# A message-passing layer on one core: node stage in two passes, section ends in the loop, one-hot offsets in PSUM

## The chip, the core and the metric

The kernel runs on one core of a Trainium2 chip. Six things work side by side on that core: TensorE (PE in the profile: matrix products and transposes, with its weight loads listed as PEld), VectorE (DVE), ScalarE (ACT), GpSimd (POOL), SyncE (SP, which here only issues transfers) and 16 DMA engines that move data between device memory and the on-chip SBUF. TensorE writes to PSUM, a small memory from which VectorE and ScalarE read the results. The engines run their own queues in order and wait for each other through semaphores.

The metric is the device time of one execution in microseconds, lower is better. Several runs are made; the median is what is compared.

## The reference

12500 nodes with 128 features, 400000 edges sorted by their target node. A pre-normalised graph layer: normalise and rectify the node features, make a message for each edge from its two ends, weight it by a small network of the edge's attributes, turn it into eight heads' scores and values, take a softmax over all edges with the same target, sum, project, and add the input.

```python
h = relu(layernorm(x))                             # 12500 x 128
msg_src = h @ w_src + b_src
msg_dst = h @ w_dst
message = msg_src[src] + msg_dst[dst]              # 400000 x 128
rad_w   = silu(silu(edge_attr_32 @ fc_w1 + fc_b1) @ fc_w2 + fc_b2) @ fc_w3 + fc_b3
message = message * edge_weight1 * rad_w
m_h     = (message @ w_sep + b_sep).reshape(E, 8, 32)
alpha, value = smooth_leaky_relu(m_h[:, :, :16]), m_h[:, :, 16:]
score   = einsum("ehk,hk->eh", alpha, alpha_dot)
att     = segment_softmax(score, dst)              # per target node and head
out     = segment_sum(value * att[..., None], dst).reshape(12500, 128) @ w_proj + b_proj
return x + out
```

## The kernel before, in words

**Node stage (L147-347).** The 12500 nodes lie in 98 tiles of 128 rows, taken four at a time (25 quads). For each quad: statistics on VectorE (`stats`, L213), normalise and rectify on ScalarE (`norm`, L227 and the lines behind it), transposes on TensorE with a copy to SBUF on VectorE (`turn`, L240-243), then products of each tile with both weight matrices side by side, 128 x 256 (`products`, L246, matmul L255), copies out of PSUM, mostly ScalarE (L261), and stores of the source product to `t_src` and of the target product to `t_dst` (L266). Between quads stand pieces of other work: `load_targets` (L176), `load_weights` (L189, one after the other on SP's queue), `fits` (L271: compares neighbouring targets, L273, and counts the falls, L276, to decide whether the fast path may be taken) and `cuts` (L302: marks where the target changes).

**The loop (`windows`, L662).** The edges are cut into 800 sections of 500, two sections make a step, 400 steps. A section's targets fall in a window of 64 nodes. Step k, an order written out by hand (`step`, L972 and on), works on several edges' stages at once: loads for later steps, the gather of source rows for step k+2, the edge network for k+2 to k, the messages of k, the scores of k-1, and, 13 steps later (LAG), the values and sums of step c = k - 13.

- `prep_load`, `prep_make`, `prep_turn` (L675-706): for every 16 steps, the source indices `idx` and the offsets `loc` of each edge's target from the first target of its section, turned by TensorE into the tile misc in PSUM and copied by VectorE to SBUF.
- `gather` (L742): POOL issues indirect transfers of 128 rows each out of `t_src` (L749), 3125 in all, into buffers `gs0` and `gs1`, three of each.
- `mlp1` (L763, matmuls L768 into the PSUM tiles `m1` and `misc`, run in two row halves of TensorE), `mlp2`, `mlp3`, `radial` (L802, VectorE L807), `sources` (L810, L819 and L822: gathered rows turned into PSUM), `message` (L825, VectorE L835), `alphas` (L838, matmul L840, VectorE L847), `scores` (L850).
- Softmax over eight steps at a time (k mod 8): running maxima up and down, each one VectorE scan of 500 columns (L875, L880), the exponentials (`softmax_exp`, L883), and their transposes into misc (`softmax_T`, L895).
- `one_hot` (L909): VectorE compares the offsets `loc` with a row of lane numbers (L913, 125 x 504) and, for the last column of each window, with the offset of the section's last target (L916, 125 x 8). `values` (L920, product L926, VectorE L928), `sums` (L933: TensorE with the one-hot as weights into misc, L937; ScalarE copy L941), then stores to a window table and to `agg`.
- In steps 40 to 239 also `load_x` and `add_x` (L952-964): input plus output bias, stored as `xb`; in the first steps the zeroing of `agg`, two transfers a step.

[...]

**After the loop (L1069-1220).** A node's edges may be split over sections, so the first and last row of every section, 1600 section ends, are combined: 13 blocks of 128 ends. Within drain steps 400 to 415 the jobs do this for all ends at once: load the ends and their maxima (L1085, L1098), scan for the common maximum (L1126), factors (L1132-1137), transposes of the ends' rows (L1143-1150), scans that sum them (L1157), quotients (L1162-1164), transposes back, and 13 scatters by POOL into `agg` (L1175).

**Final stage (L1251-1340), behind the branch.** Loads of `xb` on ScalarE's queue and of `agg` on SP's (L1268), quotients (L1279-1282), transposes (L1293), the projection (L1304), on VectorE the value bias for nodes that have edges (L1308, one instruction a tile) and the sum (L1312), and the stores of the output.

L352-660 hold a second path for other inputs, which is not taken here.

Of the kernel before, what the change touches and what calls it, by code (L numbers as in the profile page):

```python
# [30 lines left out]
P = 128  # L31
C = 128
# [24 lines left out]
def gnn_kernel(ctx: ExitStack, tc: tile.TileContext, a: dict, out: bass.AP):  # L57
# [20 lines left out]
    win = dram.tile([NS * W, ROW], F32, name="win")  # L78
    ends_d = dram.tile([1, 2 * NS + 2], I32, name="ends_d")
# [46 lines left out]
    dst_h = dst.rearrange("(k f e) -> f k e", f=2, e=SEC)  # L126
# [22 lines left out]
    with tc.tile_pool(name="node", bufs=2) as np_, tc.tile_pool(name="node1", bufs=1) as n1, \  # L149
# [15 lines left out]
        CC = E // P  # L165
        cur = n1.tile([P, CC + 1], I32, name="cur")
# [9 lines left out]
        def load_targets():  # L176

            nc.sync.dma_start(out=cur[:, 1:CC + 1], in_=dst.rearrange("(p c) -> p c", p=P))
            at = dst[CC - 1:CC]
            with nc.allow_non_contiguous_dma(reason="single targets"):  # L180
                nc.sync.dma_start(out=cur[1:P, 0:1], in_=bass.AP(at.tensor, at.offset, [[CC, P - 1], [1, 1]]))
                for f in range(2):
                    nc.sync.dma_start(out=base[:, f, :], in_=dst_h[f:f + 1, :, 0])
# [4 lines left out]
        def load_weights():  # L188
            for name, t in wt.items():  # L189
# [5 lines left out]
                nc.sync.dma_start(out=t, in_=ap)  # L195
            for f in range(2):
                for q in range(2):
                    o = (2 * q + f) * RAD
                    nc.sync.dma_start(out=w1b[o:o + RAD, f * FC:(f + 1) * FC], in_=a["fc_w1"])
                s = slice(f * FC, (f + 1) * FC)  # L200
                for q in range(2):
                    nc.sync.dma_start(out=w2b[s, q * FC:(q + 1) * FC], in_=a["fc_w2"])
                nc.sync.dma_start(out=w3b[s, :], in_=a["fc_w3"])
                nc.sync.dma_start(out=b12[s, 0:1], in_=a["fc_b1"])
                nc.sync.dma_start(out=b12[s, 1:2], in_=a["fc_b2"])
# [6 lines left out]
        hs, hTs = {}, {}  # L212
        G = 8  # L213
        def stats(t0, t1):
            for t in range(t0, t1):
# [3 lines left out]
                nc.vector.bn_aggr(mv[:n, t, :], st[:n])  # L219
            s = slice(t0, t1)  # L220
# [13 lines left out]
        def turn(i):  # L234
# [6 lines left out]
            hTs[i] = np_.tile([P, 4, P], F32, name="hT", bufs=3)  # L241
            w = (t1 - t0 - 1) * P + rows(t1 - 1)
            nc.vector.tensor_copy(hTs[i].rearrange("p u n -> p (u n)")[:, :w],
                                  pt.rearrange("p u n -> p (u n)")[:, :w])

        def products(i):  # L246
            t0, t1 = quads[i]
            hT = hTs.pop(i)
            ms = np_.tile([P, 2, 4, C], F32, name="ms", bufs=6)
            for v0 in range(t0, t1, 2):  # L250
                vs = range(v0, min(v0 + 2, t1))
                pm = nps.tile([P, 2, 2, C], F32, name="pm", bufs=4)
                for t in vs:
                    n = rows(t)
                    nc.tensor.matmul(pm[:n, t - v0], hT[:, t - t0, :n], w_nodes, start=True, stop=True)  # L255
                for n, u0, u1 in blocks(v0, vs[-1] + 1):
                    o, q = ms[:n, :, u0 - t0:u1 - t0, :].rearrange("p k j c -> p j k c"), pm[:n, u0 - v0:u1 - v0]
                    if v0 % 16 == 2:
                        nc.vector.tensor_copy(o, q)
                    else:  # L260
                        nc.scalar.copy(o, q)  # L261
            f1 = min(t1, NF)
            for k, table in enumerate((t_src, t_dst)):
                tv = table[0:NF * P, :].rearrange("(p t) c -> p t c", t=NF)
                if t0 < f1:
                    nc.sync.dma_start(out=tv[:, t0:f1, :], in_=ms[:, k, 0:f1 - t0, :])  # L266
                if t1 > NF:
                    nc.sync.dma_start(out=table[NF * P:N, :], in_=ms[:tail, k, NF - t0, :])


        def fits():  # L271
            gt = n1.tile([P, CC], BF16, name="gt")
            nc.vector.tensor_tensor(gt, cur[:, 0:CC], cur[:, 1:CC + 1], op=ALU.is_gt)  # L273
            cnt = n1.tile([P, 2], F32, name="cnt")
            nc.vector.memset(cnt, 0.0)
            nc.vector.tensor_reduce(cnt[:, 0:1], gt, AX.X, ALU.add)  # L276
# [3 lines left out]
            nc.vector.tensor_reduce(cnt[:100, 1:2], span, AX.X, ALU.add)  # L280
            tot = nps.tile([1, 1], F32, name="tot", bufs=1)
            for j in range(2):
                nc.tensor.matmul(tot, cnt[:, j:j + 1], ones[:, 0:1], start=(j == 0), stop=(j == 1))
            nc.vector.tensor_copy(bad, tot)
# [9 lines left out]


# [7 lines left out]
        def cuts():  # L303
# [16 lines left out]
            nc.vector.tensor_scalar(b_s, pb, 0.25, None, op0=ALU.mult)  # L320
            nc.vector.tensor_sub(far, eb[:, :, 1], eb[:, :, 0])
# [5 lines left out]
        stats(0, 4)  # L327
        norm(0)
        stats(4, G)
        norm(1)  # L330
        turn(0)
        for i in range(Q):
            if i % 2 == 0 and 4 * i + G < NB:
                stats(4 * i + G, min(4 * i + 2 * G, NB))
            if i + 2 < Q:
                norm(i + 2)
            if i + 1 < Q:
                turn(i + 1)
            products(i)
            if i == 5:  # L340
                load_targets()
            if i == 9:
                load_weights()
            if i == 15:
                fits()
            if i == 20:
# [314 lines left out]
    def windows():  # L661
# [5 lines left out]
        with tc.tile_pool(name="wk2", bufs=2) as sp, tc.tile_pool(name="ps", bufs=1, space=PSUM) as pp, \  # L667
                tc.manual_schedule(), ExitStack() as held:
            lp = held.enter_context(tc.tile_pool(name="ld", bufs=2))
            prep, e_g, d_g, w_g, md, gath = {}, {}, {}, {}, {}, {}  # L670
            eTs, h1s, h2s, ohT, m3, mr, mTs, als, S_all, sms, Ps, Pem, pvx, ohs, accs, xs, Ms, pms, p3s, rads = (
                {} for _ in range(20))


            def prep_load(u):  # L675
# [10 lines left out]
                prep[u] = (ri, rb)  # L686

            def prep_make(u):
                ri, rb = prep[u]
                rows = lp.tile([P, 2, P], F32, name="rows", bufs=1)  # L690
                rf = lp.tile([P, 1], F32, name="rf", bufs=1)
                nc.vector.tensor_copy(rf, rb)
                nc.vector.tensor_copy(rows[:T, 0, :], ri[:T, 0, :])
                nc.vector.tensor_scalar(rows[:, 1, 0:T], ri[:, 1, 0:T], rf, None, op0=ALU.subtract)
                prep[u] = rows

            def prep_turn(u):
                rows = prep[u]
                pt = pp.tile([P, 2, P], F32, name="misc")
                nc.tensor.transpose(pt[:, 0, 0:T], rows[:T, 0, :], ident[:T, :T])  # L700
                nc.tensor.transpose(pt[:T, 1, :], rows[:, 1, 0:T], ident)
                idx = lp.tile([P, T], I32, name="idx")
                nc.vector.tensor_copy(idx, pt[:, 0, 0:T])
# [38 lines left out]
            def gather(k, f):  # L742
                gs = lp.tile([P, TS, C], F32, name=f"gs{f}", bufs=3)
                u = k // 16
                idx, _ = prep[u]
# [17 lines left out]
            def mlp1(k):  # L763

                p1 = [pp.tile([P, 2 * T], F32, name=n) for n in ("m1", "misc")]
# [107 lines left out]
            def softmax_up(m):  # L873
                Ms[m] = sp.tile([P, 2, SEC], F32, name="M")
                nc.vector.tensor_tensor_scan(Ms[m][:, 0, :], sms[m][:, 0:SEC], S_all[m], RESTART,  # L875
                                             op0=ALU.add, op1=ALU.max)

            def softmax_down(m):
                M = Ms[m]
                nc.vector.tensor_tensor_scan(M[:, 1, ::-1], sms[m][:, SEC:0:-1], M[:, 0, ::-1], RESTART,  # L880
                                             op0=ALU.add, op1=ALU.max)
# [13 lines left out]
            def softmax_T(m):  # L895
                pt = pp.tile([T, TS, P], F32, name="misc")
                for t in range(TS):
                    nc.tensor.transpose(pt[:, t, :], Ps[m][:, t * T:(t + 1) * T], ident)
                Pem[m] = sp.tile([T, TS, MQ, H], F32, name="Pem")
                nc.scalar.copy(Pem[m].rearrange("p t q h -> p t (q h)"), pt)  # L900
# [8 lines left out]
            def one_hot(c):  # L909
                _, loc = prep[c // 16]  # L910
# [22 lines left out]
            def sums(c):  # L933
                acc = pp.tile([P, ROW], F32, name="misc")
# [12 lines left out]
            def store(c, f):  # L947
                at = nc.sync.value_load(base[0:1, f, c:c + 1])
                nc.sync.dma_start(out=agg[ds(at, W - 1), :], in_=accs[c][f * W:(f + 1) * W - 1, :])


            def load_x(i):  # L952
                xs[i] = lp.tile([P, 4, C], F32, name="xs")
# [5 lines left out]
            def add_x(i):  # L959
                t = xs.pop(i)  # L960
                for n, t0, t1 in blocks(*quads[i]):
                    u = t[:n, t0 - quads[i][0]:t1 - quads[i][0], :]
                    nc.vector.tensor_tensor(u, u, b_out[:n].unsqueeze(1).to_broadcast([n, t1 - t0, C]), op=ALU.add)
                    nc.sync.dma_start(out=xb_v[:, t0:t1, :] if n == P else xb[NF * P:N, :].unsqueeze(1), in_=u)

# [3 lines left out]
            prep_load(0)  # L969
            prep_make(0)  # L970
            prep_turn(0)
            for k in range(2):  # L972
                load_e(k)
            def step(k):
                c = k - LAG
                if has(c - 2):
# [3 lines left out]
                if k % 16 == 4 and has(k + 12):  # L980
                    prep_load((k + 12) // 16)
                if has(k + 3):
# [7 lines left out]
                if has(c - 2):  # L990
# [4 lines left out]
                if k % 16 == 8 and has(k + 8):  # L995
                    prep_turn((k + 8) // 16)
                if k % 16 == 7 and has(k + 9):
# [4 lines left out]
                if 0 <= i < Q and q == 7:  # L1002
                    add_x(i)
                if has(k + 1):
# [27 lines left out]
                if has(c):  # L1032
                    values(c, 1)
# [330 lines left out]
```

## Time and profile before

| what | value |
|---|---|
| median of 3 runs | 4316.28 us (4314.72 to 4322.2) |
| the profiled execution, its own time | 4315.26 us |
| its span (first to last instruction) | 4313.4 us |
| granted TensorE clock, mean | 0.977 |
| node stage, TensorE's first to last product | 9.0 to 108.2 us |
| first source matmul of step 15, of step 399 | 302.7, 4109.2 us |
| loads of `agg` for the final stage | 4229.7 us |
| data moved | 790.10 MB, 183 GB/s |

The page lists each engine's busy time, then the busy share in 40 equal slices of some 108 us:

```profile
PE   6679999999999999999999999999999999999974
...
DVE  7357777777777777777777777777777777777776
ACT  6335555555455455455555455454555545544521
POOL 0667777777777777777777777777777777777701
PEclk8789999999999999999999999999999999999987
DMA  5667777777777777777777777777777767777725
```

One digit is a slice, 9 meaning 90% busy or more: the first slice is the node stage, the next one or two the start of the loop, the last one the end of the section ends and the final stage; all between is the loop. In the other views a line gives the engine, the line of the kernel, the operation, and the tiles as out<-in. A group's line ends with its busy time, the mean duration in ns, and after the second bar the engine's idle time just before these instructions, with what ended it.

### The profile page before, as it was taken

The numbers are of one execution on the slowest core, as the hardware profiler recorded it, in microseconds if no ns is written. First come the engines' busy times: TensorE is split into PE (matmuls) and PEld (weight loads), VectorE is DVE, ScalarE is ACT, GpSimd is POOL, SyncE is SP. The second block draws the span as 40 slices with busy tenths as digits, with TensorE's granted clock in tenths as the row PEclk, the third lists the DMA queues.
The fourth block names the chain that finished last, engine by engine and source line by source line (L and its number), as shares of the span: only waits on it lengthen the run. The fifth ranks groups of instructions, "written<-read, shape, count | busy, mean of one in ns | idle before, by whom it ended". The sixth has DMA issues, their size and how long they took to land.

```text
span 4313.4 us, 91919 instructions
## 1 busy us (share of the span) xinstructions
PE 4065.7 (94%) x31567; PEld 2626.4 (61%) x31567; DVE 3101.8 (72%) x5980; ACT 2105.5 (49%) x4995; POOL 3037.4 (70%) x3148
## 2 busy tenths in 40 slices
PE   6679999999999999999999999999999999999974
PEld 5346666666666666666666666666666666666653
DVE  7357777777777777777777777777777777777776
ACT  6335555555455455455555455454555545544521
POOL 0667777777777777777777777777777777777701
PEclk8789999999999999999999999999999999999987
DMA  5667777777777777777777777777777767777725
GB/s 207 196 183 183 183 193 184 192 194 185 194 188 186 192 190 186 192 183 185 198 186 193 185 177 190 183 182 185 175 181 188 177 182 184 182 185 178 173 59 190
DMA packets 598603, 790.10 MB, mean 183 GB/s; under 512 B 125595, under 2 KB 475424, under 8 KB 597996
## 3 DMA queue, kind: packets, MB, share of 16 engines
q1 hardware_dynamic: 394314, 520.94, 43.1%
q0 software_dynamic: 100416, 205.45, 23.2%
q10 hardware_dynamic: 103394, 57.74, 5.1%
q8 instruction: 250, 4.10, 0.4%
q14 instruction: 229, 1.88, 0.1%
HBM read 643.48 MB, written 140.67 MB: 182 GB/s over the span
## 4 chain that ended last, share of the span: by engine, by line
PE 80%; DMA 8%; ACT 3%; DVE 3%; issue 2%; POOL 2%; SPq 1%; ACTq 0%; POOLq 0%; DVEq 0%
PE V L926 16%; PE pa L840 14%; PE misc L937 9%; PE pm L829 6%; PE p L800 6%; PE pm L819 6%; PE p L783 5%; PE m L768 5%; PE m L854 4%; PE pm L822 4%; DMA gs<-t_src,idx 4%; POOL gs L749 2%; PE m L759 2%; ACT L842 1%; DMA agg<-z 1%
## 5 line engine op out<-in xcount | busy, mean ns | idle before, releaser
L749 POOL DMA_INDIRECT gs<-t_src,idx x3125 | 3023.0, 967 | 1082.9 <-issue 778.6
L842 ACT ACTIVATE sl<-pa,c_b_a 128x500 f32<-128x500 f32 x800 | 541.8, 677 | 1004.4 <-PE pa L840 996.8
L926 PEld LDWEIGHTS V<-c_w_v,mT 128*125 128x125 f32 x6192 | 735.3, 188 | 479.8 <-DVE ohT L793 231.9
L928 DVE TENSOR_TENSOR pvx<-V,Pem 125x512 f32<-125x512 f32 x774 | 530.9, 686 | 524.2 <-PE V L926 495.5
L926 PE MATMUL V<-c_w_v,mT 128*125 128x128 f32 x6192 | 875.3, 285 | 0.2 <-DVE pvx L928 0.2
L840 PE MATMUL pa<-mT,c_w_a 128*128 128x500 f32 x1600 | 817.4, 593 | 53.8 <-DVE al L847 51.8
L847 DVE SCALAR_TENSOR_TENSOR al<-pa,sl 128x500 f32<-128x500 f32 x800 | 542.3, 678 | 239.6 <-ACT sl L842 227.0
L822 PEld LDWEIGHTS pm<-ident,gs 128*128 128x128 f32 x2350 | 418.6, 192 | 380.0 <-issue 359.5
L807 DVE SCALAR_TENSOR_TENSOR rad<-p,c_fc_b,w_b 128x500 f32<-128x500 f32 x800 | 553.3, 733 | 104.2 <-PE p L800 101.4
L835 DVE SCALAR_TENSOR_TENSOR mT<-pm,c_b_src,rad 128x500 f32<-128x500 f32 x800 | 553.2, 733 | 79.9 <-PE pm L829 66.1
L937 PE MATMUL misc<-pvx,oh 125*64 125x136 f32 x6400 | 463.7, 288 | 0.0
L937 PEld LDWEIGHTS misc<-pvx,oh 125*64 125x64 f32 x6400 | 361.1, 138 | 163.7 <-ACT eT L761 157.3
L819 PE MATMUL pm<-ident,gs 128*128 128x128 f32 (+9 forms) x2725 | 436.9, 275 | 13.1 <-DMA gs<-t_src,idx 12.7
L800 PE MATMUL p<-h,w3b 64*128 64x500 f32 x1600 | 406.5, 585 | 11.1 <-ACT h L786 11.1
L786 ACT ACTIVATE h<-p,b 128x500 f32<-128x500 f32 x400 | 326.3, 816 | 177.1 <-PE p L783 134.5
L941 ACT COPY ob<-misc 128x136 f32<-128x136 f32 x400 | 108.9, 272 | 618.3 <-PE misc L937 533.7
L822 PE MATMUL pm<-ident,gs 128*128 128x12 f32 (+30 forms) x2350 | 384.2, 244 | 16.5 <-DMA gs<-t_src,idx 15.7
L819 PEld LDWEIGHTS pm<-ident,gs 128*128 128x128 f32 (+9 forms) x2725 | 339.2, 157 | 30.2 <-DMA gs<-t_src,idx 18.3
L829 PE MATMUL pm<-ohT,m 64*128 64x500 bf16 x2400 | 325.6, 378 | 0.0
L840 PEld LDWEIGHTS pa<-mT,c_w_a 128*128 128x128 f32 x1600 | 243.1, 192 | 81.4 <-DVE al L847 65.6
L768 PE MATMUL m<-eT,w1b 64*128 64x250 f32 x800 | 276.7, 426 | 7.5 <-ACT Sp L857 6.5
L768 PE MATMUL misc<-eT,w1b 64*128 64x250 f32 x800 | 276.7, 426 | 0.0
(151 smaller groups left out, 4227.0 us busy)
## 6 DMA issues: line engine op xcount, KB each, us to landing
w_b<-in_edge_weight SPq DMA_DIRECT2D x400, 500.0 KB
d_b<-in_dst SPq DMA_DIRECT2D x400, 250.0 KB
e_t<-in_edge_attr ACTq DMA_DIRECT2D x400, 125.0 KB
gs<-t_src,idx POOLq DMA_INDIRECT x3125
sc_d<-Sp SPq DMA_DIRECT2D x200, 250.0 KB
win<-ob SPq DMA_DIRECT2D x400, 68.0 KB
agg<-ob SPq DMA_DIRECT2D x800, 33.5 KB
md<-t_dst SPq DMA_DIRECT2D x800, 32.0 KB
```

The source lines that it names most:

```text
L749: nc.gpsimd.indirect_dma_start(out=gs[:, t - t0, :], out_offset=None, in_=t_src[:, :], in_offset=bass.IndirectOffsetOnAxis(ap=idx[:, t:t + ...
L768: nc.tensor.matmul(p1[q], w1b[s, :], eTs[k][s, :], start=True, stop=True)
L800: nc.tensor.matmul(p3s[k][:, f, 0:SEC], w3b[s, :], h2s[k][s, :], start=True, stop=True)
L807: nc.vector.scalar_tensor_tensor(rad[:, s], p3[:, f, 0:SEC], b3, w_g[k][:, s], op0=ALU.add, op1=ALU.mult)
L819: nc.tensor.matmul(pms[k, f][:, a - e0:b - e0], gath[k // 16, t][:n], ident[:n, :n], start=(a == e0), stop=False, is_transpose=True, skip_ ...
L822: nc.tensor.matmul(pms[k, f][:, a - e0:b - e0], gath[k // 16, t], ident[:, a - t * P:n], start=(a == e0), stop=False, skip_group_check=True)
L829: nc.tensor.matmul(pms[k, f], m3[k][s, j, :], ohT[k][s, :], start=False, stop=(j == 2), skip_group_check=True)
L835: nc.vector.scalar_tensor_tensor(mTs[k][:, s], pms.pop((k, f)), b_n, rad[:, s], op0=ALU.add, op1=ALU.mult)
L840: nc.tensor.matmul(pa, w_a, mTs[k][:, f * SEC:(f + 1) * SEC], start=True, stop=True)
L842: nc.scalar.activation(sl, pa, AF.Silu, bias=b_a, scale=1.0)
L926: nc.tensor.matmul(V[:, t, :], mTs[c][:, o:o + T], w_v, start=True, stop=True)
L937: nc.tensor.matmul(acc[f * W:(f + 1) * W, :], ohs[c][:, f * TS + t, :], pvx[c][:, f, t, :], start=(t == 0), stop=(t == TS - 1), skip_group ...
```

## The change

Three things are changed together, with what they need.

**Node stage in two passes.** `products(i, k)` does one weight matrix (128 x 128 per tile): a first pass over all quads makes `t_src`, a second `t_dst`, out of the transposed rows kept in `x_all`. Statistics and scales are separate functions. The weights are loaded two per quad, the compare of neighbouring targets is cut into four (`falls`), the count goes through TensorE, the table `base` is copied by VectorE out of the broadcast ends instead of loaded, the first 16 steps' source indices (`idx0`) are made in the first pass, and `ids` (where the section ends scatter to) in `cuts`, which stands behind the second pass's first quad.

```diff
-            products(i)
-            if i == 5:
+            products(i, 0)
...
+            if i == 6:
+                first()
+            if i >= 3:
+                for load in (next(more, None), next(more, None)):
...
+            if 8 <= i < 12:
+                falls(i - 8)
+            if i == 13:
                 fits()
-            if i == 20:
+        for i in range(Q):
+            products(i, 1)
+            if i == 0:
                 cuts()
```

**Offsets in PSUM.** misc becomes the lower half of one 512-column tile, `bank`; `loc_turn`, at k mod 16 = 12, leaves the offsets in its upper half, and `one_hot` reads them there.

```diff
+            bank = pp.tile([P, BANK], F32, name="misc")
+            half = bank[:, 0:BANK // 2]
...
-                loc = sp.tile([T, P], F32, name="loc", bufs=3)
-                nc.vector.tensor_copy(loc, pt[:T, 1, :])
-                prep[u] = (idx, loc)
+                prep[u] = idx
+
+            def loc_turn(u):
+                o = BANK // 2 + u % 2 * P
+                locs[u] = bank[:T, o:o + P]
+                nc.tensor.transpose(locs[u], rel.pop(u), ident)
...
-                p1 = [pp.tile([P, 2 * T], F32, name=n) for n in ("m1", "misc")]
+                p1 = [pp.tile([P, 2 * T], F32, name="m1"), half[:, 0:2 * T]]
...
-            def softmax_T(m):
-                pt = pp.tile([T, TS, P], F32, name="misc")
...
+            def softmax_T(m, i):
+                pt = half[:T, :].rearrange("p (t q) -> p t q", t=TS // 2)
...
             def one_hot(c):
-                _, loc = prep[c // 16]
+                loc = locs[c // 16]
...
-                acc = pp.tile([P, ROW], F32, name="misc")
+                acc = half[:, 0:ROW]
```

As misc is half as wide, `softmax_T` is done in two halves, the first right behind `values(c, 1)`. The scans of the softmax are cut into four of 125 columns, each starting from the last value of the one before:

```diff
-                nc.vector.tensor_tensor_scan(Ms[m][:, 0, :], sms[m][:, 0:SEC], S_all[m], RESTART,
-                                             op0=ALU.add, op1=ALU.max)
+                M = Ms[m]
+                for t in range(0, SEC, T):
+                    nc.vector.tensor_tensor_scan(M[:, 0, t:t + T], sms[m][:, t:t + T], S_all[m][:, t:t + T],
+                                                 M[:, 0, t - 1:t] if t else RESTART, op0=ALU.add, op1=ALU.max)
```

`add_x` adds tile by tile, with one buffer instead of two.

**Section ends in the loop, final stage in the branch.** Block j of 128 ends is worked on from step 47 + 32 j on, in stages: loads (o = 0, four transfers on SP), maxima (2), factors (4), columns (5), totals (6) and the way out to a table in device memory (8). The quotients are no longer formed here; numerator and denominator go on to the final stage. After the loop only the last two blocks are worked on; the rows of the others are loaded back and scattered in the drain steps.

```diff
+            stages = {0: lambda g: (block_load(g), block_rows(g)), 2: block_maxima, 4: block_factors,
+                      5: block_columns, 6: block_totals, 8: block_out}
...
+                for j in (k - LATE) // SB, (k - LATE) // SB - 1:
+                    o = k - LATE - j * SB
+                    if 0 <= j < NC - 1 and o in stages:
+                        stages[o](j)
...
+            def block_columns(g):
+                w, rr = width(g), rrs.pop(g)
+                rx = sp.tile([P, C], F32, name="rx", bufs=1)
+                nc.scalar.copy(rx[:w].rearrange("p (h k) -> p h k", h=H),
+                               rr[:w, C:ROW].unsqueeze(2).to_broadcast([w, H, C // H]))
+                pt = small()
+                nc.tensor.transpose(pt[:, 0, 0:w], rr[:w, 0:C], ident[:w, :w])
+                nc.tensor.transpose(pt[:, 1, 0:w], rx[:w, :], ident[:w, :w])
...
+                for k, r in enumerate(tots[g]):
+                    nc.vector.tensor_mul(r[:, 0:w].rearrange("p (s i) -> p i s", i=2),
...
+            def block_rows_out(g, ob):
+                w = width(g)
+                po = small().rearrange("p k q -> p (k q)")
+                nc.tensor.transpose(po[:w, 0:C], tots[g][0][:, 0:w], ident)
+                nc.tensor.matmul(po[:w, C:ROW], tots[g][1][:, 0:w], ident[:, 0:P:P // H], start=True, stop=True)
+                nc.scalar.copy(ob[:w, :], po[:w, 0:ROW])
...
-            for k in range(NP, NP + LAG + 3):
+            for k in range(NP, NP + LAG + 1):
                 step(k)
-                if k - NP in jobs:
-                    jobs[k - NP]()
...
+                j = k - NP
+                if j < NC - 2:
+                    nc.sync.dma_start(out=combined(j), in_=obs_d[j * P:(j + 1) * P, :])
+                    scatter(j)
+                if j >= 4:
+                    next(x_loads, None)
```

The final stage is called at the end of this path, with the loop's PSUM tiles. All nine loads of `agg` are issued at its beginning, and the value bias moves from VectorE into the projection: a second matmul a tile, of the turned `has` by `vsel`.

```diff
-                nc.tensor.matmul(py[:n, t - t0, :], qT[:, t - t0, :n], w_proj, start=True, stop=True)
-            for t in range(t0, t1):
-                n, u = rows(t), t % XQ
-                xt = x_all[:n, t, :]
-                nc.vector.scalar_tensor_tensor(xt, v_out[:n], has[t0 // XQ][:n, u:u + 1], xt,
-                                               op0=ALU.mult, op1=ALU.add)
+                nc.tensor.matmul(py[:n, t - t0, :], qT[:, t - t0, :n], w_proj, start=True, stop=False)
+                nc.tensor.matmul(py[:n, t - t0, :], hasT[j][:m, :n], vsel[:m, t - starts[j], :],
+                                 start=False, stop=True)
```

More of the change, by code (lines that the diff above doesn't have):

```diff
@@ L262, in products @@
-            f1 = min(t1, NF)
[L263 to L268, printed above, removed]
+            pm = nps.tile([P, 4, C], F32, name="pm", bufs=4)
+            for t in range(t0, t1):
+                n = rows(t)
+                nc.tensor.matmul(pm[:n, t - t0], x_all[:, t, :n], w_nodes[:, k, :], start=True, stop=True)
@@ new lines, in gnn_kernel @@
+        with tc.tile_pool(name="fin_b", bufs=3) as fp, tc.tile_pool(name="fin1_b", bufs=1) as f1, \
+                tc.tile_pool(name="fin_ps", bufs=2, space=PSUM) as fps, tc.manual_schedule():
+            x_fin = f1.tile([P, NB, C], F32, name="x_fin")
+            for _ in load_xb(x_fin):
+                pass
+            final(fp, x_fin, lambda i: fps.tile([P, 4, P], F32, name="pt"),
+                  lambda i: fps.tile([P, 4, C], F32, name="py"), lambda: fps.tile([XQ, P], F32, name="ph"))
```

591 lines of the change are left out of this document (315 added, 276 removed).

## The prediction

> **What bounds the kernel now.** I read the page's busy times first, then the costliest groups, then the busy times by stretch.
>
> ```profile
> PE 4065.7 (94%) x31567; PEld 2626.4 (61%) x31567; DVE 3101.8 (72%) x5980; ACT 2105.5 (49%) x4995; POOL 3037.4 (70%) x3148
> ...
> L749 POOL DMA_INDIRECT gs<-t_src,idx x3125 | 3023.0, 967 | 1082.9 <-issue 778.6
> ...
> L840 PE MATMUL pa<-mT,c_w_a 128*128 128x500 f32 x1600 | 817.4, 593 | 53.8 <-DVE al L847 51.8
> ```
>
> ```profile
> 310.00:4108.00 3798.00, 3738.02 (x29614) 2401.65 (x29613) 2797.15 (x5264) 1932.57 (x4594) 2888.34 (x2984) 1.00 0.74 185
> ```
>
> The second fence is the loop alone: TensorE is busy 3738 of 3798 us (98%), so whatever makes TensorE wait there is added to the time. POOL is a second bound of nearly the same size. Its gathers start 1.273 us apart on average (0.967 and 0.30 of issue), 3125/400 = 7.81 a step, which is 9.94 us a step; from 300 to 4107 us the timeline shows no gap on POOL over 0.4 us. The first source matmuls (L819, L822) of steps 15 and 399 stand at 302.7 and 4109.2 us: 9.912 us a step. Early on the gathers run ahead (19.8 us before their use at step 15, 5 to 12 later); there, steps 40 to 79, a step takes 9.83 us. I take 9.83 as TensorE's own step and the rest as waiting for POOL.
>
> The timeline of one step around the one-hot comparison:
>
> ```profile
> 2002.96 0.69 DVE L928 TENSOR_TENSOR pvx<-V,Pem 125x512 f32<-125x512 f32 x1 [0.24 <-PE V L926]
> ...
> 2003.57 0.28 DVE L736 TENSOR_TENSOR mr<-md,m 128x128 f32<-128x128 f32 x1
> ...
> 2003.77 0.68 DVE L913 TENSOR_TENSOR oh<-lane,loc 125x504 f32<-125x504 f32 x1
> ...
> 2003.97 1.29 POOL L749 DMA_INDIRECT gs<-t_src,idx  x1 [0.30 <-issue]
> ...
> 2004.30 0.47 PE L768 MATMUL misc<-eT,w1b 64*128 64x250 f32 x1
> ...
> 2004.36 0.17 DVE L916 TENSOR_TENSOR oh<-loc,far 125x8 f32<-125x8 f32 x1
> ```
>
> Two things are to be seen. The gather under L913 takes 1.29 us instead of 0.94. And the second comparison, L916, ends at 2004.53, 0.23 us after TensorE has begun the misc half of mlp1 at 2004.30; nothing joins the two yet.
>
> The chain of waits, start and end of the run:
>
> ```profile
> 91.79 5.72 issue
> ...
> 109.34 3.58 DMA t_src<-ms
> 112.93 3.65 DMA rb<-in_dst
> 118.41 1.12 POOL gs L749
> ...
> 4129.79 6.48 DMA node<-ends_d
> ...
> 4184.00 9.76 DVE de L1163
> ...
> 4222.72 1.27 POOLq L1361
> 4226.85 2.10 DMA agg<-obs,ids
> 4229.69 10.67 DMA g<-agg
> ```
>
> The first gather stands behind the whole node stage; the loop's last work and the ends fill 4115 to 4229 us, the final stage the last 84.
>
> **The PSUM offsets.** loc leaves SBUF for the upper half of the 512-column tile whose lower half is misc. In the changed program's order of instructions and semaphores the misc half of mlp1 waits in 385 steps for that step's second comparison; in the kernel before it waits for ScalarE, and in 25 steps for the copy of loc. mlp1 keeps its place before mlp3 and radial, and the DVE order before it (pvx, mr, two comparisons) stays, so the wait is paid on TensorE. Queued behind it are mlp1's second pair, mlp3, values and alphas, whose results DVE waits for next, so the lateness closes on itself and repeats.
>
> Its size: from the rows of L916 and L768 I took, for each k mod 8 (the cycle of the softmax), how long L916 ends after misc begins: 0.28, 0.21, 0.22, 0.31, 1.36, 0.32, 0.21, 0.22 us for 0 to 7; a release from DVE to TensorE takes another 0.06 us. Seven of eight give 1.77 + 7 x 0.06 = 2.19 us. In step 4 TensorE already idles about 0.93 us before L840 behind the same late DVE (rows 0.84 to 1.03), so 1.36 + 0.06 - 0.93 = 0.49 is new. The scans (L875, L880) add a part: each of 1.19 us becomes four of 125 columns. From 64 columns at 0.344 and 500 at 1.192 us a scan of 125 is about 0.46 (estimate), four 1.85, 0.66 more; DVE has 0.24 us of slack before pvx there, so 0.42 reaches the comparison of step 3 (after the second scan 0.50 of slack covers most). Sum 3.10 us in eight steps, 0.39 a step, times 48 cycles = **150 us**. Bounds: +70, if half is covered as in step 4, to +230, if the wait also breaks the pairing of m and misc, which run together now (0.47 us each, L768). I take 150 because TensorE has no idle time to absorb it. L913 reading PSUM: 504 elements take 0.677 us now, PSUM readers of 500 take 0.678 (L847) to 0.733 (L807): 0 to +20 us, inside those bounds.
>
> [...]
>
> **What it gives POOL.** 570 gathers overlap L913 and are 0.105 us longer on average, 60 us over the run; about 2000 overlap L807 or L835, which read one operand in PSUM, and show no excess. So gathers should lose that excess, and POOL 0.15 us a step (9.79). With TensorE at 9.83 this would be worth 384 x (9.912 - 9.83) = 31 us (lower bound 19, TensorE's listed waits for gathers in the loop, 15.1 + 3.8). With TensorE at 10.2 POOL is no bound, and the gain comes only through the base I use: loop = 384 x (9.83 + 0.39 - 9.912) = -31 + 150 = +119.
> [...]
>
> **Section ends in the loop.** Each of 12 blocks puts into TensorE's queue four transposes or small matmuls, and ahead of its next work DVE and ScalarE steps. TensorE's delay is what counts: o=4 two Exps with DVE before (0.7 us), o=5 ScalarE rx, two transposes into misc, two DVE products that the next misc writer waits for (1.85), o=8 transposes and copy (0.35): 2.9 x 12 = **+35** (15, transposes alone, to 55, if every DVE step delays pvx). The four more loads of SP per block go past stores of no urgency; SP is no bound.
>
> **The start.** Pass 1 drops half the products, and ScalarE then sets a quad: 25 x 2.9 us from 9.0, and a quad for the start, end near 84 us. Both stalls go (TensorE idle 5.83 us at 66.6, behind the 3.40 and 3.41 of L273 and L276, which waited for SP, blocked from 49.7 to 66.5 by 25 weight loads of 0.6 each; and 5.72 at 91.8): the compare is cut in four, the count moves to TensorE, the weights go out two per quad. t_src and the indices are then ready, so the first gather starts near 88 instead of 118.4. Pass 2 adds 25 quads at 0.9 to 1, and cuts with its new transpose for ids, which sits behind four SP loads and a memset, some 14 us in all: the node stage ends near 121 against 108, the first e_T comes near 124 against 117.5. Gathers ahead save 10 to 14 us in the first steps, but those take 12 us each while zeros, e_t and w_b land in 11 to 14 us, which the change leaves: net **-5** (-25, if the gathers' start carries through, to +12, if pass 2 does).
>
> **The tail.** Long scans (3.3 us each) and the 9.76 us reciprocal go, and 11 scatters of 1.27 us move into the drain. g<-agg goes from 114 us after the loop's end to about 87: **-27** (0, if the agg stores and scatters on the way set it, to -55). The final stage drops 97 L1308 (27.5 us of DVE's 65.8); TensorE gets four more matmuls a quad, 20 records of 0.111 us at a clock near 0.9, 2.5 us, x 25 and a start of 12: 75 against 84, **-9** (+5 at the present clock of 0.82 to -25). Its x_fin loads ran beside g at 400 to 430 GB/s; now ScalarE's queue issues them from step 404 on, where DMA moves 51 GB/s (stretch 4108 to 4229) and ScalarE is busy 21 of 121 us, so I cost them at nothing.
>
> **Sum** against the span: 4313.4 - 5 + 119 + 35 - 27 - 9 = 4426; the run itself lies 2 us above its span and 1 below the median of 4316.28. I say 4427.
>
> **Rivals.**
> 1. *The wait costs nothing* (the other side): DVE runs ahead of TensorE once POOL no longer paces the step, so that L916 ends before misc is issued. Then 4313.4 - 5 - 31 + 35 - 36 = 4276. For it: DVE is only 72% busy. Against: pvx starts 0.24 us after TensorE's own values, so DVE cannot run ahead. It decides where L916 ends less than 0.06 us before misc; with the wait under 0.1 us a step the kernel is faster.
> 2. *The wait costs double*: weight loads behind it are held too, and m and misc no longer pair (0.47 us of overlap a step): 150 + 94 (a half of 0.47 x 400) gives about 4520. For it: m's second matmul is queued behind the first misc one. Against: m's first runs on during the wait.
> 3. *Half hidden*, as in step 4: +70 in place of +150, about 4347.
> 4. *The reading of PSUM frees no gather*: at 10.2 us a step nothing changes; it only matters with rival 1, which then ends near 4307.
>
> **How the numbers follow.** The forecast has 0.67, rival 1 0.17 (with 4 inside it), rival 2 0.10, rival 3 0.06. The likeliest case's own range is 4350 to 4490, from the wait's bounds and a part of the others; the range for 8 in 10 is 4290 to 4500. A difference of 0.2% (9 us) is what can be told from none. Faster 0.17, same 0.02, slower 0.81.
>
> **What would show it.** In the changed kernel's profile: waits of TensorE's misc matmul (now L834) for DVE L988, some 385 times 0.25 to 0.3 us; steps of 10.2 us; gathers of 0.95 us with POOL now waiting for buffers; a first gather near 88 us; g loads about 90 us after the loop. No such wait, or steps under 9.9, and the forecast is wrong.

## The result and the profile after

| | before | after |
|---|---|---|
| median | 4315.65 us (4314.72 to 4322.2, 4 runs) | 4600.43 us (4596.06 to 4607.61, 4 runs) |
| span of the profiled execution | 4313.4 us | 4594.1 us |
| mean granted TensorE clock | 0.977 | 0.960 |

The ratio is 1.0658, with a 95% interval of 1.064 to 1.0676: slower, as forecast, but by 285 us where 111 had been forecast. Four stages, cut at the first source matmul of steps 15 and 399 and where the loads of `agg` begin (4229.7 and 4404.1 us), hold all of it:

| stage | before, us | after, us | change | forecast |
|---|---|---|---|---|
| start to step 15 | 302.7 | 333.7 | +31.0 | -5 |
| steps 15 to 399 | 3806.5 | 3966.7 | +160.2 | +154 (119 + 35) |
| to the loads of `agg` | 120.5 | 103.7 | -16.8 | -27 |
| final stage | 83.7 | 190.0 | +106.3 | -9 |

The page of the changed kernel, first busy times, then the granted clock in 40 slices of 115 us:

```profile
PE 4351.6 (95%) x31999; PEld 2831.6 (62%) x31999; DVE 3139.5 (68%) x6356; ACT 2134.2 (46%) x5101; POOL 2983.3 (65%) x3147
...
PEclk9789999999999999999999999999999999999955
```

The last two slices stand at 5: TensorE runs at half clock (0.50) through the whole final stage. The busy times of that stage alone (span; busy PE, PEld, DVE, ACT, POOL; clock; DMA share; GB/s), before and after:

```profile
4229.70:4313.40 83.70, 42.34 (x294) 40.26 (x294) 65.78 (x164) 15.57 (x26) 0.00 (x0) 0.83 0.63 235
```

```profile
4404.10:4594.10 190.00, 162.12 (x499) 116.92 (x499) 40.20 (x67) 16.67 (x34) 0.00 (x0) 0.50 0.18 70
```

VectorE lost its 25 us as planned, and TensorE took over as the bound with 162 us of work. The timeline of TensorE there shows the price of one matmul, which the trace lists as two records:

```profile
4426.25 0.80 PE L1367 MATMUL pa<-c_w_proj,qT 128*128 128x128 f32 x2
4426.98 0.79 PE L1368 MATMUL pa<-vsel,hasT 12*128 12x128 f32 x2
4427.70 1.11 PE L1354 MATMUL pm<-ident,q 128*128 128x128 f32 x4
```

Matmuls start 0.72 us apart, so 0.36 us a record, whether the weights have 128 rows or 12. In the kernel before, at half clock too in its first two quads (0.50 in the slice from 4240 us), records of one shape started 0.213 us apart and, once the clock was released (1.00 in the slice from 4248 us), 0.112:

```profile
4245.01 1.06 PE L1293 MATMUL pt<-ident,q 128*128 128x128 f32 x4
4245.87 1.64 PE L1304 MATMUL py<-c_w_proj,qT 128*128 128x128 f32 x8
...
4249.35 1.06 PE L1304 MATMUL py<-c_w_proj,qT 128*128 128x128 f32 x8
4250.25 0.60 PE L1293 MATMUL pt<-ident,q 128*128 128x128 f32 x4
```

In the loop, the step shown before, now with the offsets in PSUM:

```profile
2103.73 0.67 DVE L985 TENSOR_TENSOR oh<-lane,misc 125x504 f32<-125x504 f32 x1
...
2104.31 0.48 PE L834 MATMUL m<-eT,w1b 64*128 64x250 f32 x1
2104.32 0.17 DVE L988 TENSOR_TENSOR oh<-misc,far 125x8 f32<-125x8 f32 x1
...
2104.54 0.47 PE L834 MATMUL misc<-eT,w1b 64*128 64x250 f32 x1
2104.63 0.37 PE L834 MATMUL m<-eT,w1b 64*128 64x250 f32 x1
...
2104.84 0.58 PE L866 MATMUL p<-h,w3b 64*128 64x500 f32 x1
2104.86 0.37 PE L834 MATMUL misc<-eT,w1b 64*128 64x250 f32 x1
```

m starts at 2104.31, misc only at 2104.54, 0.05 us after the second comparison ended; the two began together before. From m's start to the first product of values it takes 1.80 us (median of 319 steps between 700 and 4000 us), against 1.46 before. The list of TensorE's waits in the loop shows little of this (us in total, times, longest):

```profile
PE misc L834 <- DVE oh L988: 45.2, 49, 1.7
PE misc L1009 <- DVE oh L988: 19.3, 9, 7.6
PE misc L1098 <- ACT Pem L972: 7.3, 12, 0.7
PE misc L764 <- ACT obk L1118: 6.3, 11, 0.6
```

49 waits of some 385: in the others m's matmul was still running while misc waited, so TensorE counted as busy. These waits, which ended before the work ahead of them did, are not listed as idle time, and yet they delayed everything behind them: 1.80 us against 1.46.

In some rounds of runs the kernel before itself took 5760 to 5865 us instead of about 4315, for a reason that is not known; from those rounds only stages and the ratio to the kernel before are read.

### The profile page after: what moved, and what is told of

It is laid out like the page before. It is cut to its first block, busy times and chain, and to the rows that moved or that the text cites. A ratio compares the mean times of both kernels' runs of the same rounds, so it can differ in the third digit from the quotient of the medians.

```text
span 4594.1 us, 93435 instructions
## 1 busy us (share of the span) xinstructions
PE 4351.6 (95%) x31999; PEld 2831.6 (62%) x31999; DVE 3139.5 (68%) x6356; ACT 2134.2 (46%) x5101; POOL 2983.3 (65%) x3147
## 5 line engine op out<-in xcount | busy, mean ns | idle before, releaser
L815 POOL DMA_INDIRECT gs<-t_src,idx x3125 | 2968.0, 950 | 1315.4 <-issue 749.2
L888 PEld LDWEIGHTS pm<-ident,gs 128*128 128x128 f32 x2350 | 418.2, 192 | 360.4 <-issue 360.4
L866 PE MATMUL p<-h,w3b 64*128 64x500 f32 x1600 | 552.2, 599 | 6.3 <-ACT h L852 6.3
L1009 PE MATMUL misc<-pvx,oh 125*64 125x136 f32 x6400 | 461.6, 287 | 21.4 <-DVE oh L988 20.0
L1009 PEld LDWEIGHTS misc<-pvx,oh 125*64 125x64 f32 x6400 | 359.5, 137 | 184.2 <-ACT eT L827 153.7
L888 PE MATMUL pm<-ident,gs 128*128 128x12 f32 (+30 forms) x2350 | 381.4, 242 | 0.0
L885 PEld LDWEIGHTS pm<-ident,gs 128*128 128x128 f32 (+9 forms) x2725 | 338.3, 157 | 12.9 <-DMA gs<-t_src,idx 8.8
L834 PE MATMUL misc<-eT,w1b 64*128 64x250 f32 x800 | 273.3, 422 | 50.9 <-DVE oh L988 45.2
L834 PE MATMUL m<-eT,w1b 64*128 64x250 f32 x800 | 276.9, 427 | 4.9 <-ACT Sp L923 4.0
L849 PE MATMUL p<-h,w2b 64*64 64x250 f32 x3200 | 263.3, 400 | 18.2 <-DVE rad L873 18.2
## 6 DMA issues: line engine op xcount, KB each, us to landing
e_t<-in_edge_attr ACTq DMA_DIRECT2D x400, 125.0 KB
```

The lines of the kernel that those rows point to most:

```text
L815: nc.gpsimd.indirect_dma_start(out=gs[:, t - t0, :], out_offset=None, in_=t_src[:, :], in_offset=bass.IndirectOffsetOnAxis(ap=idx[:, t:t + ...
L834: nc.tensor.matmul(p1[q], w1b[s, :], eTs[k][s, :], start=True, stop=True)
L866: nc.tensor.matmul(p3s[k][:, f, 0:SEC], w3b[s, :], h2s[k][s, :], start=True, stop=True)
L885: nc.tensor.matmul(pms[k, f][:, a - e0:b - e0], gath[k // 16, t][:n], ident[:n, :n], start=(a == e0), stop=False, is_transpose=True, skip_ ...
L888: nc.tensor.matmul(pms[k, f][:, a - e0:b - e0], gath[k // 16, t], ident[:, a - t * P:n], start=(a == e0), stop=False, skip_group_check=True)
L1009: nc.tensor.matmul(acc[f * W:(f + 1) * W, :], ohs[c][:, f * TS + t, :], pvx[c][:, f, t, :], start=(t == 0), stop=(t == TS - 1), skip_group ...
```

## The experiments

**The loop: is it the wait?** Two ways to take its cause away. The first copies the offsets to SBUF:

```diff
-                locs[u] = bank[:T, o:o + P]
-                nc.tensor.transpose(locs[u], rel.pop(u), ident)
+                nc.tensor.transpose(bank[:T, o:o + P], rel.pop(u), ident)
+                locs[u] = sp.tile([T, P], F32, name="loc", bufs=2)
+                nc.vector.tensor_copy(locs[u], bank[:T, o:o + P])
```

> The changed kernel with the offsets copied from PSUM to SBUF by VectorE every 16 steps, and the one-hot comparison reading them there; misc is still half a tile. Theory W (TensorE's misc half of mlp1 waits for the second comparison): steps 15 to 399 fall from 10.33 to 10.00 to 10.10 us, bounded by POOL and by the section ends, the whole by 90 to 130 us, and the gathers' excess returns (from 19 to about 70 us). Rival (the loop's loss is the split scans and the section ends): steps stay above 10.25, the whole falls by under 30 us.

Measured 4440.05 us (one run; the kernel before beside it 4318.59): 160 us less. Steps 15 to 399 take 9.936 us against 10.330; m and misc begin together again, and m to values takes 1.46 us:

```profile
2018.29 0.47 PE L835 MATMUL m<-eT,w1b 64*128 64x250 f32 x1
2018.30 0.47 PE L835 MATMUL misc<-eT,w1b 64*128 64x250 f32 x1
```

The gathers' excess, the sum over all of them of what each takes beyond its usual 0.944 us, returned, from 18.8 to 65.5 us. (The same edit had been run once before, with 5992.18 us beside a kernel before of 5790.33; its loop is not read.) The second leaves the offsets in PSUM and puts other work into the wait:

```diff
-                if has(k + 2):
-                    mlp1(k + 2)
                 if has(k):
                     mlp3(k)
+                if has(k + 2):
+                    mlp1(k + 2)
```

> The changed kernel with mlp3 issued before mlp1 on TensorE, so that 0.9 us of other work lies between the sources and the misc half of mlp1, and the wait for the second comparison falls into it. Theory W: seven steps of eight lose their 0.25 to 0.31 us, 0.24 us a step, steps fall from 10.33 to about 10.1 us, the whole by about 90 us. Rival (TensorE's matmuls slow down for another reason, as clock or pairing): no change.

4446.99 us, steps of 9.942: more than expected, since step 4 of eight gained too (between 700 and 4000 us its mean fell from 11.94 to 11.37) and step 3, with the late scans, gained 0.69. Theory W holds both ways: what cost the time is the wait, not the place of the offsets.

**The scans**, each one instruction again:

> The changed kernel with each softmax scan in one instruction of 500 columns. Theory S (four of 125 make the values and the comparison late in one step of eight): that step falls by 0.4 us, the whole by 15 to 25 us. Rival (slack hides them): the whole falls by under 5 us.

4558.72 us, 42 less; step 3 of eight falls from 10.92 to 10.50 (medians), the 0.42 of theory S. The rest is in step 4, where the section ends' columns fall from 3.8 to 2.0 us a block. The gathers' excess rose from 18.8 to 53.6 us: the 167 gathers that overlap a whole scan are 0.25 us longer on average, the 218 that overlap one of the short scans in the changed kernel 0.02. Both kinds of scan read two operands in SBUF, so that alone does not set what a gather loses; why cutting them helps POOL is not shown.

**The start.** In the last ten quads of pass 1 a quad takes 3.44 us (4.40 in most of those before), in one cycle, as the timeline of the changed kernel shows:

```profile
88.71 0.58 ACT L261 COPY ms<-pm 128x512 f32<-128x512 f32 x1 [1.31 <-PE pm L254]
...
89.19 1.65 ACT L234 ACTIVATE h<-x_all,shift,rstd 128x128 f32<-128x128 f32 x4
...
89.74 1.48 PE L243 MATMUL pt<-ident,h 128*128 128x128 f32 x4 [1.07 <-ACT h L234]
...
91.06 1.06 PE L254 MATMUL pm<-w_nodes,x_all 128*128 128x128 f32 x8
...
92.15 0.58 ACT L261 COPY ms<-pm 128x512 f32<-128x512 f32 x1 [1.12 <-PE pm L254]
```

ScalarE idles 1.1 to 1.3 us ahead of each copy, waiting for products that stand behind transposes that wait for the norm that ScalarE does after the copy of the quad before. The edit:

```diff
+            if i + 2 < Q:
+                norm(i + 2)
             products(i, 0)
             if i + 4 < Q:
                 stats(*quads[i + 4])
-            if i + 2 < Q:
-                norm(i + 2)
...
-            if i == 0:
+            if i == 13:
                 cuts()
```

> The changed kernel with two edits in the node stage: the norm of quad i+2 stands ahead of the products of quad i on ScalarE again, and cuts comes behind the second pass's quad 13 instead of its quad 0. Theory N (each quad of pass 1 costs 3.44 us because ScalarE's norm waits behind the copy of products that wait for the transposes of the norm before; and cuts stops TensorE for 12 us): a quad falls to 2.6 to 2.9 us, the first gather comes near 97 instead of 112.6 us, the stage ends near 118 instead of 146, the first sources near 132 instead of 159, the whole falls by 20 to 28 us. Rival (the first steps are set by transfers alone): step 15 stays near 330 us.

4570.64 us, 30 less: pass 1 ends at 84.4 us, the first gather is at 89.9, step 0 at 131.5 and step 15 at 307.7 (the changed kernel: 109, 112.6, 159.2, 333.7; the kernel before, from the gather on: 118.4, 125.0, 302.7). The stop of TensorE in cuts stayed, 8.3 us at its new place, so nearly all of the gain is that of norm; the two were not run apart.

**The final stage.** First the value bias back on VectorE, as in the kernel before.

> The changed kernel with the value bias of the final stage back on VectorE (97 scalar_tensor_tensor) and without the twelve-row matmuls. Theory A (the twelve-row matmuls between the full ones stop the weight loads from overlapping, 0.36 us a record against 0.21 at the same clock, and so TensorE's clock is never released): the granted clock rises to about 0.9 in the final stage as in the kernel before, the stage falls from 190 us to 75 to 90 us, the whole from 4600 to about 4495 us. Rival B (the stage merely starts cold, with nine loads at once and the loop's PSUM tiles, whatever the matmuls): the clock stays at 0.50, half the products go, the stage takes about 115 us, the whole about 4525.

The stage took 83.3 us at a clock of 0.77 (beside a kernel before of 5790 us). The same kernel once more:

> The changed kernel with the value bias of the final stage back on VectorE and nothing else, on another chip. Theory A: the final stage takes 83 us against 190, the clock there is about 0.85, the whole falls by 107 us to about 4493.

81.7 us at 0.81, so the stage is nearly the same; the whole took 4481.27 (the kernel before beside it: 4309.49). Then the second matmul kept, but padded with zeros to 128 rows:

```diff
-            has[i] = fp.tile([P, XQ], F32, name="has")
+            has[i] = fp.tile([P, P], F32, name="has")
...
-        vsel = fp.tile([XQ, XQ, C], F32, name="vsel", bufs=1)
+        vsel = fp.tile([P, XQ, C], F32, name="vsel", bufs=1)
```

> The changed kernel with the value bias still a second matmul a tile, but with has and vsel padded with zeros from 12 to 128 rows: as many matmuls, all of one shape. Theory A: records take about 0.21 us cold, the clock is released within 10 us, records then 0.11 us, the stage takes 80 to 100 us, the whole about 4500. Rival C (twice as many matmuls are too many by themselves): the stage stays at 150 us or more and the clock at 0.50.

The stage took 98.0 us with as many matmuls as the changed kernel's 190:

```profile
5952.00:6050.00 98.00, 69.29 (x499) 67.06 (x499) 40.89 (x74) 16.80 (x34) 0.00 (x0) 0.83 0.35 136
```

So rival C, the number of matmuls, falls. What about the shape is it? Grouped, four full matmuls and then four of twelve rows (in this order the two products are no longer added in every tile; number and sizes are the same):

> The changed kernel with the twelve-row matmuls kept, but the four of a quad behind its four full ones, so that the shape changes twice a quad instead of eight times. Theory A1 (it is the alternation of shapes): weight loads overlap again, the clock is released, the stage takes 85 to 105 us. Theory A2 (it is the few rows, TensorE's activity counts as too small): the clock stays at 0.50 and the stage takes 110 to 160 us.

126.2 us at 0.65: the time lies in the range of A2, the clock between the two. At half clock the first two records after a change to twelve rows start 0.351 and 0.375 us after the ones ahead of them, 0.30 us more than two of 0.213; after the change back, 0.346 and 0.267, 0.19 more. All others start 0.213 apart, twelve rows or not. The clock rose in stretches and fell again (1.00 in the slice of 4 us from 5976 us, 0.58 in the next), and in others TensorE was busy 4.00 of 4.00 us at 0.50, as in this slice:

```profile
5984.00:5988.00 4.00, 4.00 (x18) 3.55 (x18) 0.07 (x1) 0.59 (x1) 0.00 (x0) 0.50 0.19 70
```

So the alternation (A1) sets the price of a record. What holds the clock back in this run, the few rows (A2) or the two changes a quad that are left, it can't tell. Sixty-four rows, still alternating:

> The changed kernel with has and vsel padded with zeros to 64 rows, alternating with the full matmuls. Theory A1 (a change of shape between neighbours stops the weight loads): records take about 0.36 us at half clock and the clock stays at 0.50: a stage of about 190 us. Theory A2 (few rows count as little activity): with 64 of 128 rows the clock is released at least in part, a stage of 100 to 130 us.

190.4 us at 0.50, and matmuls again 0.72 us apart: the price is that of the change, not of the twelve rows. And twelve rows, alternating, without the gaps ahead of the turn of `has`:

> The changed kernel with its twelve-row matmuls, alternating, but the quotients one quad earlier and the turn of has one quad later, so that TensorE has no gap of 1.9 us at every third quad. Theory G (the gaps keep the clock halved): the clock is released, the stage falls to 100 us or less. Theory A (the matmuls themselves): the clock stays at 0.50 and the stage falls only by the eight gaps, 10 to 25 us, to 165 to 180 us.

174.0 us. The busy times of that stage, in two stretches:

```profile
5982.74:6012.74 30.00, 30.00 (x93) 21.58 (x92) 7.11 (x9) 2.60 (x5) 0.00 (x0) 0.50 0.11 41
6012.74:6052.74 40.00, 40.00 (x125) 29.12 (x124) 9.59 (x14) 4.03 (x8) 0.00 (x0) 0.50 0.11 40
```

TensorE is busy 70 of 70 us and stays at 0.50: theory G falls. Shown is that a change of rows cost up to 0.30 us at half clock, and that the clock was not released in a stretch full of such changes, with 12 rows or with 64 (0.50 over the whole stage in both). What in a change holds the clock back is not shown: the weight loads took 0.23 us each in the changed kernel's stage (116.92 over 499), and no run separates their part. Changes alone do not do it when they are rarer: in the loop matmuls of 64 rows (L834) follow those of 128 (L888), and the clock there is 0.99 (700 to 4000 us).

**What is left when it is mended.** Five edits together (mlp3 before mlp1, whole scans, the two of the start, the first indices' load earlier and their turn later, the bias on VectorE):

> The changed kernel with five edits together: mlp3 before mlp1, scans whole, norm ahead of the products and cuts behind quad 13, the first indices' load moved to quad 4 and their turn to quad 9, the value bias on VectorE. If the single effects add up (4600 - 153 - 20 - 34 - 107): about 4290; from the stages (step 15 at 305, steps of 9.92, 187 us from step 399 on): about 4302 us, 0.3% under the kernel before. If the loop is bound by POOL as before: 4310 or more.

4293.86 us, ratio 0.996 (0.9946 to 0.9973) to the kernel before.

> The same with the section ends' columns one step later (o=6), totals at o=7 and the way out at o=10, away from the steps that use misc for the transposes of the softmax and of the indices. If their cost in the loop (2.1 + 1.0 us a block) is the wait for ScalarE's copies out of misc, it falls to about 1.2 us a block, 20 us less than the run before it: 4280 us. If it is the transposes and copies themselves: no change.

4286.28 us, 0.994 (0.9927 to 0.9954). The section ends fall from 2.6 (1.59 + 1.03) to 1.9 us a block (0.47 + 1.12 + 0.29, in the steps o = 5, 6 and 10), where 1.2 had been expected if the wait was all of it.

> The same as the second, but with the value bias as a second matmul of 128 zero-padded rows, the quotients one quad earlier and the turn of has one quad later than they were. If TensorE at full clock is faster than VectorE here: the final stage takes about 72 us against 83, the whole about 10 us less than the run before it. If the clock falls again in the gaps: 95 us, the whole 12 us more.

4275.30 us, 0.9913 (0.9896 to 0.9931), the fastest. Its final stage:

```profile
4205.90:4276.30 70.40, 57.61 (x499) 56.90 (x499) 40.34 (x74) 16.74 (x34) 0.00 (x0) 0.91 0.50 190
```

The run before it, with the bias on VectorE, took 81.5 us there. So the bias belongs on TensorE after all, in 128 rows and with the turn of `has` moved.

**Are the offsets in PSUM worth anything?** The fastest version with the offsets in SBUF and mlp1 back in its place:

> The fastest version so far (4275 us), but with the offsets copied to SBUF and compared there, and mlp1 before mlp3 as in the kernel before. If reading the offsets in PSUM is worth something once its wait is hidden (the gathers' excess rises from 63 to about 100 us and POOL bounds the step): 10 to 40 us slower than that version. If not: within 5 us of it.

0.9993 of the kernel before (0.9955 to 1.0031), and in the next try 1.002 (0.9987 to 1.0054), both beside a kernel before of about 5790 us. The third:

> The same kernel a third time, for a chip on which the kernel before takes about 4310 us: 0.9913 of it, within 0.1%, if the offsets in PSUM are worth nothing; 0.2 to 0.9% more if they are.

4280.58 us, 0.9922 (0.9909 to 0.9936), against 0.9913 (0.9896 to 0.9931) for PSUM: the intervals overlap. Steps take 9.922 against 9.899 us, 9 us over the loop, which the totals can't tell from nothing. Last, split scans in the fastest version:

> The fastest version so far (0.9913 of the kernel before), but with the four-part scans of the change. Theory P (one long scan with both inputs in SBUF lengthens gathers, the excess was 63 us with whole scans and 26 with split ones, and POOL bounds the step): excess near 26 us, 5 to 20 us faster than with whole scans. Theory T (TensorE bounds it, and late values cost 0.1 to 0.4 us in one step of eight): 5 to 20 us slower.

0.9939 (0.9909 to 0.9969), beside a kernel before of 5788 us, in the round in which the version with the offsets in SBUF and whole scans had 1.002: there the offsets in PSUM and the split scans together were worth 0.8%. The excess of the gathers was 17 us against 72. Which of the two edits did it, and whether it pays where the kernel before takes 4310 us, stays open.

## Why the prediction was right in sign and wrong in size

The sign was no luck: the loop alone, for the wait that was named, is 160 us slower.

- **The PSUM offsets: right in mechanism, and somewhat lucky in size.** "0.39 a step" for the wait; undoing it gave 10.330 - 9.936 = 0.394. But in steps without a block of section ends it gave 0.344 (10.190 - 9.846), 132 us; some 18 us more are blocks that the wait made dearer. The wait is that of L834 for L988 and is paid in full, which rivals 1 and 3 denied; the doubling of rival 2 didn't come: m and misc lost their pairing, but misc then ran beside m's second matmul and mlp3's first. No run kept the offsets in PSUM and left out the semaphore behind the wait, so whether it is needed there is not shown. The scans' 0.42 in step 3 was met to the hundredth; it is felt only through the wait (without it step 3 takes 10.22 on average against 10.15 before).
- **POOL: right, and worth little.** Gathers of 0.950 us, excess 18.8 against 74.2 us (33.7 in a second run with the same loop, the one with the bias on VectorE); at 10.3 us a step it bought nothing, as rival 4 had it, and with the wait hidden at most 9 us instead of 31.
- **Section ends in the loop: mis-sized.** Only 11 of the "12" blocks fall into these steps, the twelfth comes behind step 399. "2.9 x 12 = +35" was 3.2 x 11 = 35 without the wait (2.19 at o = 5, 1.03 at o = 8, from steps with and without a block) and 4.85 x 11 = 53 with it: the columns fall into the step in which misc also carries the softmax's transposes, and the way out into the one ahead of the indices' turn. The loop's sum closes with -25 (9.846 against 9.912, forecast -31) + 132 + 53 = 160; that 154 came so near is partly errors of opposite sign.
- **The start: the step that failed is "ScalarE then sets a quad: 25 x 2.9 us".** I took ScalarE's load for its period. The diff moved norm behind the products, which closed a cycle over ScalarE and TensorE of 3.44 us, and 4.40 in earlier quads, and the turn of `idx0` added a stop of 4.4 us; with norm back, pass 1 ended at 84.4 us, where the forecast had 84, and the gather came at 89.9 (88). That gathers ahead help the first steps, "-5" net, fell too: with the gather 28 us earlier than before, step 15 was still 5 us later.
- **The tail** gave 17 of the 27 us. In it TensorE waited 20.0 us, in ten waits, for the second comparison (L1009 for L988; the kernel before has no such wait there), and 12.9 us for the last block's rows, which are loaded (L1066, 4395.7 us) behind the stores on SP's queue. Which of them holds the missing 10 us was not tested.
- **The final stage: the step that failed, and the largest miss, is "20 records of 0.111 us at a clock near 0.9, 2.5 us".** A row of the kernel before was carried over to matmuls that stand between others of another shape. Measured 0.36 us a record in the products at a clock of 0.50, 6.5 us of TensorE a quad (162.12 / 25). The upper bound, +5, took the clock from before as given; 115 us of the 168 that the span lies above the sum are here.

The forecast's range ended at 4500; none of its rivals held TensorE as the bound of the final stage.

## What to carry to other kernels

Moving a short operand into the upper half of a PSUM tile whose lower half TensorE writes turned a read that nothing waited for into a wait (1.80 us from m to values, against 1.46): look at what TensorE writes there next, and put other matmuls between. When an added matmul is priced from a row of the trace, look at the row counts of its neighbours: at half clock a record took 0.213 us among its own shape and 0.36 between others, and padding with zeros to 128 rows was cheaper here than a small matmul (98 against 190 us, and 70 against 174 with the turn of `has` moved). And an order that is changed by one line in a software pipeline has to be followed around the cycle, engine by engine, before a load is taken for a period.

## What the hardware showed that I had not expected

Matmuls of 12 or 64 rows alternating with 128 take 0.36 us a record at half clock, those of one shape 0.213, and in the run without gaps the granted clock stays at 0.50 for 160 us, in which the profile has TensorE busy for 158.5 (from 5962.74). With matmuls of one shape it was released within 4 us of unbroken products in the kernel before (from 4243.15; 0.61 in the slice from 4244 us, 1.00 from 4248) and within some 6 us in pass 2 of the changed kernel (from 120.7; 0.50 in the slice from 122 us, 0.91 from 126). TensorE was busy with hardly a gap in all three stretches; by what the clock is granted is not shown.
